# A decoder layer on one core: where the token numbers of the second choice are written

## The chip, the cores and the metric

The kernel runs on one core of a Trainium2 chip. The metric is the device time of one execution in microseconds (us); lower is better. The core's engines run side by side, each working through its own queue of instructions: TensorE (PE in the profile, with its weight loads as PEld), VectorE (DVE), ScalarE (ACT), GpSimd (POOL) and SyncE (SP), which issues DMAs. Engines wait for each other by semaphores.

## The reference

The input `x` is 64 sequences of 128 tokens with 256 features each. One layer does three things, with a layer normalization after each: a selective-scan block, a cross attention without softmax against `ctx_1024`, and a mixture of experts. Only the last matters here:

```python
shared = ...                                   # one expert that every token uses
probs = jax.nn.sigmoid(logits)                 # 8 experts
scores, indices = jax.lax.top_k(probs, TOP_K)  # the best 2
scores = scores / jnp.sum(scores, axis=-1, keepdims=True)
...
g = jax.nn.silu(jnp.einsum('th,ehi->tei', xf, gate_w))
u = jnp.einsum('th,ehi->tei', xf, up_w)
combined = jnp.einsum('tei,eih,te->th', g * u, down_w, w)
return shared + combined.reshape(b, s, h)
```

Every token thus has a first and a second choice of expert, and a weight for each.

## The kernel before

All values are 32-bit floats. The sequences are handled in 16 groups of 4 (`GB`), counted from 0; a group is 512 tokens, laid out as 128 partitions by 4 sequences.

For each group the program runs `front` and `scan` (the selective scan), then, while the next group's `front` and `scan` run, `after` (output projection, layernorm, cross attention, layernorm) and `route`. A weaver takes steps of these generators in turn, together with `early_shared` (the shared expert for an earlier group) and `routed` (tiles of rows for the eight routed experts). When the groups are through, the remaining routed tiles, the shared expert of groups 7 to 13 and the final sums follow.

`route` sorts tokens to experts. It computes the rank of each expert for each token ("gt", "same", "rank"), the position of each token in its expert's list ("pre", "count", "pc", "ad", "at", "index"), and the two weights ("wk2", "tot"). A token's features then go out twice, once for each choice, as rows of 258 numbers (`DX`): 256 features, in column `D` a number that says where its result is to be written later, in column `D + 1` the weight. `rows[0]` is the buffer in which `after` has already made x2; it comes from a ring of two and is called "x" or "x2" in the profile. `rows[1]` is "row1", a pool tile with one buffer, called "row" in the profile. (The profile also has a small tile "row" in the lists of tiles, L1139 to L1144, that has nothing to do with it.) Line 1016 copies x2 into row1 on ScalarE, line 1037 writes column `D` of both rows from a constant "slot", line 1038 writes column `D + 1`. Line 1042 scatters the rows to the DRAM tensor "xs": four indirect DMAs for each choice, issued by GpSimd, eight for each group.

The number in column `D` of a token at partition p of sequence b is 256 b + 2 p for the first choice and one more for the second.

The expert stage fetches tiles of 256 or 128 such rows (`fetch`, L1183), multiplies them with the gate and up weights (L663), forms "hid" (L1221, L1222), multiplies with the down weights (L672) and scatters the results to "ys" by the number in column `D` (L1235).

The order in which each engine gets its instructions isn't the program's. A planner simulates the engines, takes whatever it holds to be ready, and among ready ones the earlier in the program; buffers are handed out in the same way, and it puts in the semaphores. So an instruction with few dependencies can stand far ahead of its neighbours in the source. Within one engine the resulting order is then fixed: an instruction that waits holds up all behind it.

Other lines that the prediction names: L630 to L640 are the layernorm (statistics on VectorE, "rstd" on GpSimd, "shift" on VectorE, the scaling on ScalarE); L649 and L651 transpose; L672 is `project_rows`, used for the output projection from "sz" among others; L788 to L826 are the scan, with "d", "cj" and "mt" made on VectorE; L840 to L847 are its last products, with "sz" as their result; L868 adds the residual; L1065 and L1073 belong to the shared expert; L1080 stores x2 with the shared expert's part to "x_rows", from which it is read back at the end.

Of the kernel before, what the change touches and what calls it, by code (L numbers as in the profile page):

```python
# [11 lines left out]
F32 = mybir.dt.float32  # L12
AF = mybir.ActivationFunctionType
ALU = mybir.AluOpType
AX = mybir.AxisListType

P = 128
L = 128
D = 256
# [10 lines left out]
GB = 4  # L30
# [467 lines left out]
def shared_decay(K):  # L498

    with ExitStack() as ctx:
        _shared_decay(ctx, K)


def _shared_decay(ctx, K):
    tc, nc = K.tc, K.tc.nc
    NG = K.x.shape[0] // GB
# [8 lines left out]
    const = ctx.enter_context(tc.tile_pool(name="masks", bufs=1))  # L518
# [53 lines left out]
    with nc.allow_non_contiguous_dma(reason="a vector over partitions, once"):  # L572
        for j in range(NB):
# [15 lines left out]
    nc.vector.memset(order[:, 1, :], 1.0)  # L589
    count = const.tile([P, NE], F32, name="count")  # L590
    nc.vector.memset(count, 0.0)
    slot = const.tile([P, NG * GB, 2], F32, name="slot")
    nc.gpsimd.iota(slot, pattern=[[2 * L, NG * GB], [1, 2]], base=0, channel_multiplier=2,
                   allow_small_or_imprecise_dtypes=True)


# [71 lines left out]
    def project_rows(ps, src, w, cols):  # L668

        chunks = len(src)  # L670
        for k in range(chunks):
            nc.tensor.matmul(ps, lhsT=src[k], rhs=w[:, k, cols], start=(k == 0), stop=(k == chunks - 1))  # L672
# [268 lines left out]
    def wrote(g, ins):  # L941

        tc.declare_no_dep(ins, group="scatters", reason="other rows")
        for k in range(len(BATCHES)):
            if needs(k) <= g:
                tc.declare_no_dep(ins, group=f"fetches{k}", reason="other rows")
        for group in ("scatters", f"scatters{g}"):
            tc.add_to_no_dep_group(group, ins)
        writers.append((g, ins.name))
# [13 lines left out]
    def turned(x2):  # L963
        x2T = two.tile([P, KD, T], F32, name="x2T")
        transposed(x2T, x2)
        return x2T

    def route(g, st):

        x2 = st["x2"]  # L970
        x2T = turned(x2)
        yield

        pr = pm.tile([P, GB, NE], F32, name="pm")
        for b in range(GB):
            project_rows(
                pr[:, b, :], [x2T[:, k, b * L : (b + 1) * L] for k in range(KD)], rw, slice(0, NE)
            )
        pb = small.tile([P, GB, NE], F32, name="pb", bufs=1)
        nc.vector.tensor_tensor(pb, pr, rb.unsqueeze(1).to_broadcast([P, GB, NE]), ALU.add)  # L980
        nc.scalar.activation(pb, pb, AF.Exp, scale=-1.0)
        yield
        nc.vector.tensor_scalar(pb, pb, 1.0, None, ALU.add)
        nc.vector.reciprocal(pb, pb)
        pj = pb.unsqueeze(2).to_broadcast([P, GB, NE, NE])
        pe = pb.unsqueeze(3).to_broadcast([P, GB, NE, NE])
        gt = small.tile([P, GB, NE, NE], F32, name="gt", bufs=1)
        eq = small.tile([P, GB, NE, NE], F32, name="same", bufs=1)
        nc.vector.tensor_tensor(gt, pj, pe, ALU.is_gt)
        nc.vector.tensor_tensor(eq, pj, pe, ALU.is_equal)  # L990
        nc.vector.tensor_tensor(
            eq.rearrange("p b e j -> p b (e j)"), eq.rearrange("p b e j -> p b (e j)"),
            bef.rearrange("p e j -> p (e j)").unsqueeze(1).to_broadcast([P, GB, NE * NE]), ALU.mult,
        )
        nc.vector.tensor_tensor(gt, gt, eq, ALU.add)
        rank = small.tile([P, GB, NE], F32, name="rank", bufs=1)
        nc.vector.tensor_reduce(rank, gt, AX.X, ALU.add)
        sel = small.tile([P, GB, NE], F32, name="sel", bufs=1)
        nc.vector.tensor_scalar(sel, rank, 1.5, None, ALU.is_lt)


        pre = small.tile([P, GB, NE], F32, name="pre", bufs=1)
        nc.vector.tensor_copy(pre[:, 0, :], count)
        for b in range(1, GB):
            nc.vector.tensor_tensor(pre[:, b, :], pre[:, b - 1, :], sel[:, b - 1, :], ALU.add)
        nc.vector.tensor_tensor(count, pre[:, GB - 1, :], sel[:, GB - 1, :], ALU.add)
        yield
        yield
        pc = pm.tile([P, GB, NE], F32, name="pm")
        pcf = pc.rearrange("p b e -> p (b e)")  # L1010
        nc.tensor.matmul(pcf, lhsT=upto, rhs=sel.rearrange("p b e -> p (b e)"), start=True, stop=False)
        nc.tensor.matmul(pcf, lhsT=ones, rhs=pre.rearrange("p b e -> p (b e)"), start=False, stop=True)
        yield

        rows = [st["row"], one.tile([P, GB, DX], F32, name="row1")]
        nc.scalar.copy(rows[1][:, :, 0:D], x2)
        mk = small.tile([P, GB, 2, NE], F32, name="mk", bufs=1)
        nc.vector.tensor_tensor(
            mk, rank.unsqueeze(2).to_broadcast([P, GB, 2, NE]),
            order.unsqueeze(1).to_broadcast([P, GB, 2, NE]), ALU.is_equal,  # L1020
        )
        ad = small.tile([P, GB, NE], F32, name="ad", bufs=1)
        nc.vector.tensor_tensor(ad, pc, begin.unsqueeze(1).to_broadcast([P, GB, NE]), ALU.add)
        ma = small.tile([P, GB, 2, NE], F32, name="ma", bufs=1)
        nc.vector.tensor_tensor(ma, mk, ad.unsqueeze(2).to_broadcast([P, GB, 2, NE]), ALU.mult)
        at = small.tile([P, GB, 2], F32, name="at", bufs=1)
        nc.vector.tensor_reduce(at, ma, AX.X, ALU.add)
        index = small.tile([P, GB, 2], mybir.dt.int32, name="index", bufs=2)
        nc.vector.tensor_copy(index, at)
        nc.vector.tensor_tensor(ma, mk, pb.unsqueeze(2).to_broadcast([P, GB, 2, NE]), ALU.mult)  # L1030
        wk2 = small.tile([P, GB, 2], F32, name="wk2", bufs=1)
        nc.vector.tensor_reduce(wk2, ma, AX.X, ALU.add)
        tot = small.tile([P, GB], F32, name="tot", bufs=1)
        nc.vector.tensor_reduce(tot, wk2, AX.X, ALU.add)
        nc.vector.reciprocal(tot, tot)
        for k in range(2):
            nc.vector.tensor_copy(rows[k][:, :, D], slot[:, g * GB : (g + 1) * GB, k])
            nc.vector.tensor_tensor(rows[k][:, :, D + 1], wk2[:, :, k], tot, ALU.mult)  # L1038
        yield
        for k in range(2):  # L1040
            for b in range(GB):
                s = nc.gpsimd.indirect_dma_start(  # L1042
                    out=xs, in_=rows[k][:, b, :], in_offset=None,
                    out_offset=bass.IndirectOffsetOnAxis(ap=index[:, b, k : k + 1], axis=0),
                )
                wrote(g, s.ins)
        yield
        if g in LATE:
            nc.sync.dma_start(out=x2_rows[g].rearrange("p (b d) -> p b d", d=D), in_=x2)
        st["x2T"] = x2T  # L1050
# [242 lines left out]
    def second_half(g, st):  # L1293
        yield from after(g, st)
        yield
        yield from route(g, st)
        for k, (groups, *_) in enumerate(BATCHES):
            if groups == g + 1:
                tile_list(k)

    states = [{} for _ in range(NG)]
    rows = routed()
# [219 lines left out]
```

## Time and profile before

| what | us |
|---|---|
| median of 3 timed runs | 2166.24 |
| their range | 2158.91 to 2171.72 |
| the profiled execution | 2132.54 |
| its span, first to last instruction | 2130.8 |
| TensorE busy, groups 1 and 2 (125 to 287 us) | 145.84 of 162 |
| TensorE busy, groups 9 to 14 (852 to 1449 us) | 579.67 of 597 |
| TensorE busy, routed tiles after the groups (1640 to 1931 us) | 278.70 of 291 |

The profile's stretches show three regimes. In the first groups, which have no routed tiles to work on yet, TensorE idles some 10% of the time. From group 8 on, the routed tiles fill it. At the end, routed tiles and the shared expert run alone.

Lines of the profile read like this: line of the code, engine, operation, tiles (written <- read), shape; then the number of such instructions, their busy time and mean, and how long the engine stood idle ahead of them and what ended that idle time. A gap on TensorE costs time as such; on another engine it does only if TensorE has to wait in turn.

### The profile page before, as it was taken

Reading aid. Unit: us, or ns where it says so; the run is one execution under the profiler, and the core shown is the slowest. Engines: PE = TensorE matmul, PEld = TensorE weight load, DVE = VectorE, ACT = ScalarE, POOL = GpSimd, SP = SyncE. Lnnn points to the kernel's source line nnn. Section 1 sums busy time; section 2 is a strip of 40 time slices with the busy share of each in tenths; the row PEclk is TensorE's granted clock in tenths of the full one; section 3 lists DMA queues with packets and bytes.
Section 4 is the critical chain, followed back from the end, with each engine's and each line's share of the span. In section 5 each row is a group of like instructions: output and inputs, shape, how many; then the busy total and the mean of one; then the engine's idle time right before and its main releaser. Section 6 shows DMA issues by size and latency. Waiting matters only on the chain.

```text
span 2130.8 us, 25083 instructions
## 1 busy us (share of the span) xinstructions
PE 1963.9 (92%) x8748; PEld 1419.6 (67%) x8748; DVE 1001.5 (47%) x2426; ACT 775.9 (36%) x1254; POOL 462.9 (22%) x669
## 2 busy tenths in 40 slices
PE   4789899999898999999999999999989999888987
PEld 1546565666666676867676767777666888885544
DVE  3665665765555565545555654554431111113563
ACT  2444344342424343444444353535221222222332
POOL 3021221211202131313131222213131222221010
PEclk9899999999999999999999999999999999999999
DMA  4111111412212133424243333334243456844660
GB/s 123 33 49 32 49 58 40 157 40 75 90 60 90 60 125 114 140 75 164 80 149 115 114 120 109 97 102 150 80 156 129 160 193 206 312 144 158 211 213 32
DMA packets 97384, 245.13 MB, mean 115 GB/s; under 512 B 22400, under 2 KB 58880, under 8 KB 88288
## 3 DMA queue, kind: packets, MB, share of 16 engines
q1 hardware_dynamic: 74128, 188.17, 26.8%
q0 software_dynamic: 17616, 52.46, 7.3%
q10 hardware_dynamic: 5504, 2.81, 0.5%
q8 instruction: 71, 1.16, 0.2%
q14 instruction: 65, 0.53, 0.1%
HBM read 202.62 MB, written 54.93 MB: 121 GB/s over the span
## 4 chain that ended last, share of the span: by engine, by line
PE 70%; DVE 9%; DMA 7%; ACT 5%; POOL 4%; issue 4%; SPq 0%; DVEq 0%; POOLq 0%; ACTq 0%
PE gu L663 24%; PE pm L672 17%; PE pm L663 15%; PE pm L717 2%; POOL xs L1042 2%; PE gu L672 2%; PE pm L649 2%; PE pm L840 2%; DMA xs<-row,index 1%; PE pm L914 1%; PE pm L927 1%; PE pm L1203 1%; DMA x_back<-x_rows 1%; POOL rstd L635 1%; DMA routed_w<-in_ffn_dram 1%
## 5 line engine op out<-in xcount | busy, mean ns | idle before, releaser
L663 PE MATMUL gu<-rows_T,routed_w 128*128 128x256 f32 (+1 forms) x2496 | 507.3, 354 | 9.0 <-ACT rows_T L1205 5.5
L663 PEld LDWEIGHTS gu<-rows_T,routed_w 128*128 128x128 f32 x2496 | 416.5, 191 | 75.6 <-issue 20.1
L672 PE MATMUL pm<-routed_w,hid 128*128 128x256 f32 x1080 | 252.3, 381 | 13.7 <-DVE hid L1222 12.8
L663 PE MATMUL gu<-x2T,shared_w 128*128 128x512 f32 x512 | 238.9, 614 | 16.4 <-DVE hid L1222 7.7
L1222 DVE TENSOR_TENSOR hid<-hid,gu 128x512 f32<-128x512 f32 x135 | 91.9, 685 | 335.0 <-PE gu L663 323.5
L663 PE MATMUL pm<-xnT,w_in_s 128*128 128x512 f32 x512 | 244.7, 604 | 0.7 <-ACT xnT L653 0.7
L672 PEld LDWEIGHTS pm<-routed_w,hid 128*128 128x128 f32 x1080 | 200.7, 190 | 49.4 <-DVE hid L1222 17.5
L1235 POOL DMA_INDIRECT ys<-rows_out,to x135 | 133.7, 991 | 346.8 <-ACT rows_out L1234 310.3
L663 PEld LDWEIGHTS gu<-x2T,shared_w 128*128 128x128 f32 x512 | 97.4, 196 | 132.0 <-issue 108.0
L1221 ACT ACTIVATE hid<-gu 128x512 f32<-128x512 f32 x135 | 80.5, 596 | 260.2 <-PE gu L663 259.9
L701 DVE SCALAR_TENSOR_TENSOR xc<-pm,cw,xc 128x508 f32<-128x508 f32 (+2 forms) x192 | 140.6, 740 | 65.6 <-ACT xc L696 62.5
L663 PEld LDWEIGHTS pm<-xnT,w_in_s 128*128 128x128 f32 x512 | 97.6, 195 | 86.1 <-issue 74.8
L1234 ACT ACTIVATE rows_out<-pm,wt 128x256 f32<-128x256 f32 x135 | 57.8, 471 | 266.3 <-PE pm L672 245.6
L635 POOL TENSOR_TENSOR rstd<-var,mhalf 128x4 f32<-128x4 f32 x64 | 68.1, 1065 | 346.6 <-DVE var L633 179.1
L672 PE MATMUL pm<-w_out_s,sz 128*128 128x256 f32 x512 | 121.7, 394 | 13.2 <-DVE sz L847 13.1
L672 PE MATMUL gu<-shared_w,hc 128*128 128x256 f32 x512 | 118.9, 382 | 5.5 <-DVE hc L1065 5.5
L672 PEld LDWEIGHTS pm<-w_out_s,sz 128*128 128x128 f32 x512 | 99.9, 198 | 31.9 <-DVE sz L847 16.3
L672 PEld LDWEIGHTS gu<-shared_w,hc 128*128 128x128 f32 x512 | 95.1, 190 | 27.4 <-DVE hc L1065 8.7
L1042 POOL DMA_INDIRECT xs<-x,index x64 | 66.2, 1034 | 126.3 <-DVE row L1038 49.5
L696 ACT ACTIVATE xc<-pm,cb,cw 128x512 f32<-128x512 f32 x64 | 49.5, 773 | 110.0 <-PE pm L663 110.0
L640 ACT ACTIVATE x<-x,shift,rstd 128x256 f32<-128x256 f32 x128 | 67.9, 590 | 57.3 <-DVE shift L637 57.3
L1205 ACT COPY rows_T<-pm 128x512 f32<-128x512 f32 (+1 forms) x78 | 41.2, 528 | 130.3 <-PE pm L1203 130.3
(225 smaller groups left out, 2628.4 us busy)
## 6 DMA issues: line engine op xcount, KB each, us to landing
routed_w<-in_ffn_dram SPq DMA_DIRECT2D x78, 1536.0 KB
picked<-ys SPq DMA_DIRECT2D x16, 1024.0 KB
rows_in<-xs SPq DMA_DIRECT2D x57, 258.0 KB
xt<-in_x_dram POOLq DMA_DIRECT2D x16, 512.0 KB, 4.3
cT<-in_ctxT_dram POOLq DMA_DIRECT2D x16, 512.0 KB, 4.2
cq<-chunks SPq DMA_DIRECT2D x16, 512.0 KB
x_rows<-x SPq DMA_DIRECT2D x16, 512.0 KB
x_back<-x_rows SPq DMA_DIRECT2D x16, 512.0 KB
```

The costliest lines, as they stand in the source:

```text
L635: nc.gpsimd.tensor_tensor(rstd, var, mhalf, ALU.pow)
L640: nc.scalar.activation(dst[:, b, :], src[:, b, :], AF.Identity, bias=shift[:, b : b + 1], scale=rstd[:, b : b + 1])
L649: nc.tensor.transpose(ps[:, b * L : (b + 1) * L], src[:, b, k * P : (k + 1) * P], ident)
L663: nc.tensor.matmul(ps, lhsT=w[:, k, col : col + P], rhs=src[:, k, :], start=(k == 0), stop=(k == KD - 1),)
L672: nc.tensor.matmul(ps, lhsT=src[k], rhs=w[:, k, cols], start=(k == 0), stop=(k == chunks - 1))
L696: nc.scalar.activation(xcf[:, c, :], ps, AF.Identity, bias=cb[:, c : c + 1], scale=cw[:, c, TAPS - 1 : TAPS],)
L701: nc.vector.scalar_tensor_tensor(xc[:, c, :, s:], ps3[:, :, : L - s], cw[:, c, TAPS - 1 - s : TAPS - s], xc[:, c, :, s:], ALU.mult, ALU.add,)
L1042: s = nc.gpsimd.indirect_dma_start(out=xs, in_=rows[k][:, b, :], in_offset=None, out_offset=bass.IndirectOffsetOnAxis(ap=index[:, b, k : k ...
L1221: nc.scalar.activation(hc, psg, AF.Silu)
L1222: nc.vector.tensor_tensor(hc, hc, psu, ALU.mult)
L1234: nc.scalar.activation(y[:, j, :], ps[:, j, :], AF.Copy, scale=wt[:, j : j + 1])
L1235: s = nc.gpsimd.indirect_dma_start(out=ys, in_=y[:, j, :], in_offset=None, out_offset=bass.IndirectOffsetOnAxis(ap=to[:, j : j + 1], axis=0),)
```

## The change

The constant "slot" holds the numbers of the first choice alone. They are copied into column `D` of `rows[0]` ahead of the copy of x2. ScalarE's copy into row1 takes 257 columns in place of 256, so that it carries the first choice's number along, and VectorE adds 1 to it in row1. What is computed stays the same.

```diff
-    slot = const.tile([P, NG * GB, 2], F32, name="slot")
-    nc.gpsimd.iota(slot, pattern=[[2 * L, NG * GB], [1, 2]], base=0, channel_multiplier=2,
+    slot = const.tile([P, NG * GB], F32, name="slot")
+    nc.gpsimd.iota(slot, pattern=[[2 * L, NG * GB]], base=0, channel_multiplier=2,
                    allow_small_or_imprecise_dtypes=True)
...
         rows = [st["row"], one.tile([P, GB, DX], F32, name="row1")]
-        nc.scalar.copy(rows[1][:, :, 0:D], x2)
+        nc.vector.tensor_copy(rows[0][:, :, D], slot[:, g * GB : (g + 1) * GB])
+        nc.scalar.copy(rows[1][:, :, 0 : D + 1], rows[0][:, :, 0 : D + 1])
...
         nc.vector.reciprocal(tot, tot)
+        nc.vector.tensor_scalar(rows[1][:, :, D], rows[1][:, :, D], 1.0, None, ALU.add)
         for k in range(2):
-            nc.vector.tensor_copy(rows[k][:, :, D], slot[:, g * GB : (g + 1) * GB, k])
             nc.vector.tensor_tensor(rows[k][:, :, D + 1], wk2[:, :, k], tot, ALU.mult)
```

## The prediction

> **What bounds the kernel now.** I read the page first, then the table of waits over all engines, then the waits of TensorE alone, then the lines that the diff touches, and last the timeline around each of them.
>
> The page's first part says who is busy:
>
> ```profile
> PE 1963.9 (92%) x8748; PEld 1419.6 (67%) x8748; DVE 1001.5 (47%) x2426; ACT 775.9 (36%) x1254; POOL 462.9 (22%) x669
> ```
>
> TensorE has work for 92% of the span of 2130.8 us, so about 167 us is all that any other engine can still be costing. A gain has to come out of those 167 us. The table of waits shows one wait that belongs to a line of the diff (columns: who waited, for whom, total us, times, longest us):
>
> ```profile
> DVE hid L1222 <- PE gu L663: 323.5, 88, 7.2
> ...
> DVE row L1037 <- DMA xs<-row,index: 137.9, 15, 14.0
> ```
>
> The first row is VectorE waiting for the bottleneck, which is healthy. The second is not: a copy of four numbers for each partition holds VectorE still for 137.9 us, 15 times, until the scatter DMAs that read "row" have landed. L1037 copies the token numbers from the constant "slot" into column D of both rows. The constant is ready from the start, so nothing but the buffer holds this copy back, and it stands far ahead of the routing it belongs to: in group 2 it runs at 240.9 us, while "mk" (L1018) of that group runs at 296.1. "row1" has one buffer, which the eight scatters of the group before are still reading. TensorE's own waits on VectorE:
>
> ```profile
> PE pm L788 <- DVE d L784: 19.0, 12, 4.9
> PE pm L672 <- DVE sz L847: 13.1, 5, 6.1
> ...
> PE pm L840 <- DVE mt L826: 12.4, 4, 5.7
> ```
>
> To see which of these are caused by L1037 I went through the timeline at each of the 15 places. Groups are counted from 0. Group 1, group 6 and group 9 (start, us, engine, line, idle before and its releaser):
>
> ```profile
> 156.38 0.96 POOL L1042 DMA_INDIRECT xs<-row,index  x1 [0.30 <-issue]
> 158.97 0.17 DVE L1037 COPY row<-slot 128x4 f32<-128x4 f32 x1 [5.60 <-DMA xs<-row,index]
> 159.05 0.69 DVE L847 TENSOR_TENSOR sz<-sz,xc 128x512 f32<-128x512 f32 x1
> 159.79 1.65 PE L672 MATMUL pm<-w_out_s,sz 128*128 128x256 f32 x3 [5.41 <-DVE sz L847]
> ```
>
> ```profile
> 571.51 1.89 PE L663 MATMUL gu<-rows_T,routed_w 128*128 128x256 f32 x8
> 579.00 1.41 PE L840 MATMUL pm<-mt,xd 128*128 128x128 f32 x5 [5.60 <-DVE mt L826]
> ...
> 578.06 0.17 DVE L1037 COPY row<-slot 128x4 f32<-128x4 f32 x1 [10.05 <-DMA xs<-row,index]
> 578.16 0.69 DVE L826 TENSOR_TENSOR mt<-mt,pm 128x512 f32<-128x512 f32 x1
> ```
>
> ```profile
> 890.69 5.35 PE L663 MATMUL gu<-rows_T,routed_w 128*128 128x256 f32 x24
> ...
> 894.42 0.17 DVE L1037 COPY row<-slot 128x4 f32<-128x4 f32 x1 [12.44 <-DMA xs<-row,index]
> ```
>
> In groups 1 and 6 the instruction right behind the copy in VectorE's queue is the one TensorE needs next. In group 9 the stall is longer still, but TensorE is filled with matmuls of the routed experts throughout.
>
> **What the Trainium skill says.** "TensorE: Matmul & The Clock Gate", table at the top: VectorE's and ScalarE's queues are strict FIFO. The trace agrees: L847 does not run while L1037 waits. "DMA: Bandwidth & Descriptors", section on the SWDGE path: a fixed cost of about 2.0 us, most of it the receipt for the last byte. Here the last scatter of group 1 is issued at 156.38 and releases the copy at 158.97, 2.6 us later. "Perfetto Trace Analysis", section Optimization Strategy: find the gaps of the bound engine and what blocks them; the sum below is made that way.
>
> **The change, part by part.**
>
> *Removed: the copy into "row" column D.* Its wait for the scatters goes with it. The other copy, into "x" (the group's own row, two buffers), stays, and is as early as before: its waits are 2.2 us in all (1.7 and 0.5). What the removal is worth to TensorE I take from TensorE's gaps at the stalls (us): group 1, 5.41; group 2, 6.14; group 3, 2.12 and 0.83 (transposes at L649 waiting for the layernorm that began behind the copy); group 5, 0.68 and 0.70; group 6, 5.60; group 7, 5.74; group 15, 0.83. Sum 28.05. In group 4 TensorE waits 3.70 us right after the stall, but for the fetch of routed rows, which SyncE issues after the scatters; I count nothing. In groups 8 to 14 the seven stalls sum to 74.6 us and TensorE waits for none of them: nothing there either. So of 137.9 us, 28 us are on the path.
>
> What is late next? Group 1: L847 would start at 153.37 and end at 154.06; TensorE is done with its earlier work at 159.79 - 5.41 = 154.38, so the gap closes entirely. Group 6: "mt" would be ready at 568.7, and TensorE comes free at 573.4: closed. Group 3: the second half of the projection ends at 320.3; in the trace the transpose starts 3.88 us after that half's L868, so at 324.2, and TensorE is busy to 325.2: closed. I keep 1 us back for the places where VectorE and TensorE end within 0.4 us of each other (five, at 0.2 us each).
>
> *Moved: the copy of x2 to row1 on ScalarE (L1016)* reads one column more and now also depends on the copy from "slot". It grows from 128x1024 to 128x1028 elements: 4/1024 of its 1047 ns, 16 times, 0.07 us. Its new wait costs nothing: the copy from "slot" runs 47 to 149 us earlier (group 2: 219.7 against 286.8). It was already waiting for the scatters of the group before (two semaphore instructions of 38 ns ahead of it), and these have landed at least 41 us before. It cannot run ahead as L1037 did, since it reads x2, which the layernorm finishes just then.
>
> *Added: the +1 on VectorE.* One TENSOR_SCALAR of 128x4, 0.17 us like L763, in place of one COPY of 0.17 us (median 172 ns): nothing. Its wait is new: it needs the ScalarE copy. If it stands as early as possible, it holds VectorE until that copy ends. In groups 0 to 2 VectorE has at most two small operations there (L729, L752), and in groups 3 to 14 it has nothing to do then: group 8's copy ends at 853.45 and VectorE's next instruction, "hid", starts at 854.59 after an idle 2.77 us, waiting for TensorE. Over the groups this reserve is 1.1 to 4.4 us. Cost between 0 and, if ScalarE's copy comes some 2 us later than this reserve in every group, 2 x 16 = 32 us; I take 0. Behind it would be queued "hc", "hid" and "tok", which TensorE's down projections and ScalarE wait for. If it stands where the program puts it, after the reciprocal, the copy is done 10 us earlier and there is no wait at all.
>
> *Moved: nothing on SyncE or POOL.* The scatters still wait for L1038. The constant is half as wide, at start-up only.
>
> Sum: -28.05 + 0.07 + 1 = -27 us, from 2132.5 (the profiled execution) to 2105.5. The timed runs shown have a median of 2166.24 (2158.91 to 2171.72), 1.6% above the profiled one; the gaps are waiting times, so I carry the difference in us: 2166.2 - 27 = 2139.
>
> **What I can't see.** The order on each engine is laid out by a planner, and another instruction list gives another order. Downwards: the small gaps before L788 (19.0 us, 4.9 of them in the first group) may close too: 28 + 14 = 42 us, 2124; runs of one kernel spread by 6 us around their median, so I go to 2120. Upwards, the rivals set the end.
>
> **Rivals.**
>
> *A, the stall goes and stays gone:* 2139. For it: the seven places above, with the next instruction named at each.
>
> *B, another copy takes its place:* the copy "x" from "slot" is also unbound and stands near the old one (group 5: 480.8, held 0.89 us by the x_rows store; the other at 486.9). With VectorE earlier, it may come before that store has landed; group 2's store takes 5.7 us to land (213.95 to 219.63). At 3 us in each of groups 2 to 8, 21 of the 28 us come back: 2166 - 7 = 2159. Against it: in groups 1 to 5 and 8 it stands ahead of the old copy, so no stall of that group shields it, and in 6 and 7 the store itself is issued behind the old stall (579.48), so it moves forward with it. That the change does not lift the wait at all belongs here: the buffer's scatters would then hold ScalarE, but long after they landed.
>
> *C, slower: VectorE is held by the +1.* Place: the end of the layernorm of x2 in each group, if the planner puts the +1 early and ScalarE takes the copy behind other work. Price: a hold that reaches TensorE like those of groups 6 and 7, 5.6 us; in seven groups 39 us, so 2166 - 28 + 39 = 2177. It decides from 28/16 = 1.75 us lost on TensorE in every group. Against it: the reserve above, and that stalls of 12 us in groups 8 to 14 cost nothing.
>
> **How the numbers follow.** A change below 0.5% (11 us) is what a measurement of this kernel can't tell from none. A 0.75, B 0.13, C 0.12. Of A, 0.73 lie beyond 0.5% and 0.02 within; of B, 0.04 beyond and 0.09 within; of C, 0.11 slower and 0.01 within. Faster 0.77, same 0.12, slower 0.11. The range is 2120 to 2161: A with its unknown order, and most of B; C and the tails are left out.
>
> **What would show it.** After: no row "DVE row <- DMA xs<-row,index" in the waits; TensorE's waits for "sz" at about 0.2 us (13.1 less 12.93) and for "mt" at about 1.1 (12.4 less 11.34); TensorE's busy time unchanged at about 1964 us and its share up to 93%; groups 8 to 14 still about 99 us long, groups 1 to 7 shorter by 28 us together. Wrong would be: a wait of VectorE for the ScalarE copy row<-x, longer waits for x_rows, or gaps on TensorE at places that have none now.

## The result

Timed beside each other, the changed kernel takes 2130.05 us (median of 4 runs, 2126.02 to 2133.43) and the kernel before 2162.57 us (4 runs, 2155.16 to 2171.72). The ratio is 0.9847, 95% interval 0.9802 to 0.9892: 32.5 us less, where 27 were forecast. The profiled execution took 2126.02 us, its span is 2124.3.

After the change, the first part of the page:

```profile
PE 1962.0 (92%) x8748; PEld 1421.2 (67%) x8748; DVE 1005.6 (47%) x2426; ACT 775.6 (37%) x1254; POOL 462.2 (22%) x669
```

After the change, from the table of waits over all engines (who waited, for whom, total us, times, longest us):

```profile
DVE hid L1223 <- PE gu L663: 317.8, 94, 7.2
...
DVE row L1037 <- ACT row L1017: 23.6, 15, 3.7
```

And from the waits of TensorE alone:

```profile
PE gu L663 <- ACT rows_T L1206: 25.6, 15, 7.2
PE pm L788 <- DVE d L784: 21.3, 13, 4.9
...
PE pm L840 <- DVE mt L826: 1.1, 2, 0.6
```

VectorE's 137.9 us of waiting for the scatters are gone. In their place stands a wait of 23.6 us, that of the +1 (now L1037) for ScalarE's copy (now L1017). On TensorE the wait for "sz" is gone and that for "mt" is down from 12.4 to 1.1 us. But there is a new row at the top: TensorE waits 25.6 us for "rows_T", against 5.5 before. It looks as if the change had paid with a new wait. Several of the experiments below ask whether it has.

The order of instructions is the same in both kernels on TensorE, ScalarE, GpSimd and SyncE, from first to last. On VectorE the only differences are that the sixteen early copies "row" from "slot" are gone and sixteen +1 have come, each right behind ScalarE's copy. So the planner did not answer with another order; what changed is when things run.

Here the span is cut at the starts of ScalarE's copy to row1 of groups 0, 7 and 14, into groups 1 to 7, groups 8 to 14, and the rest. The columns are the stretch in us, its length, then busy us (and number of instructions) of PE, PEld, DVE, ACT and POOL, the granted clock (the share of its full clock that TensorE was given), the DMA share and GB/s. Before:

```profile
125.00:749.00 624.00, 584.87 (x2409) 386.67 (x2410) 369.76 (x886) 244.57 (x381) 123.28 (x141) 0.98 0.22 68
749.00:1449.00 700.00, 681.49 (x3137) 510.51 (x3136) 373.44 (x907) 310.95 (x480) 178.62 (x243) 1.00 0.36 116
1449.00:2130.00 681.00, 618.13 (x2939) 477.93 (x2937) 198.66 (x488) 177.73 (x333) 134.64 (x237) 0.97 0.48 165
```

After:

```profile
122.00:710.00 588.00, 573.40 (x2412) 379.75 (x2413) 370.98 (x886) 244.53 (x380) 122.80 (x140) 0.99 0.23 72
710.00:1438.00 728.00, 691.42 (x3139) 517.44 (x3137) 376.12 (x907) 312.11 (x483) 179.12 (x243) 0.98 0.34 112
1438.00:2124.00 686.00, 618.78 (x2937) 480.44 (x2936) 199.53 (x489) 176.90 (x332) 134.62 (x237) 0.97 0.48 164
```

Groups 1 to 7 are 36 us shorter, more than the 28 us forecast for them, and groups 8 to 14 are 28 us longer, where no difference was forecast. Two questions follow: why is the gain in the early groups larger than the gaps that were counted, and what do the late groups pay for?

### The profile page after: what moved, and what is told of

Same layout as the page of the kernel before. It is cut to its first block, busy times and chain, and to the rows that moved or that the text cites. A ratio compares the mean times of both kernels' runs of the same rounds, so it can differ in the third digit from the quotient of the medians.

```text
span 2124.3 us, 25079 instructions
## 1 busy us (share of the span) xinstructions
PE 1962.0 (92%) x8748; PEld 1421.2 (67%) x8748; DVE 1005.6 (47%) x2426; ACT 775.6 (37%) x1254; POOL 462.2 (22%) x669
## 4 chain that ended last, share of the span: by engine, by line
PE 71%; DVE 9%; issue 5%; ACT 5%; DMA 5%; POOL 2%; another core or an unknown queue 1%; SPq 0%; POOLq 0%; DVEq 0%; ACTq 0%
PE gu L663 24%; PE pm L672 16%; PE pm L663 15%; PE gu L672 3%; PE pm L840 2%; PE pm L717 2%; PE pm L649 2%; PE pm L914 1%; PE pm L927 1%; PE pm L1204 1%; POOL rstd L635 1%; PE pm L833 1%; PE pm L802 1%; DMA ys<-rows_out,to 1%
## 5 line engine op out<-in xcount | busy, mean ns | idle before, releaser
L663 PE MATMUL gu<-rows_T,routed_w 128*128 128x256 f32 (+1 forms) x2496 | 514.4, 358 | 28.4 <-ACT rows_T L1206 25.6
L672 PE MATMUL gu<-shared_w,hc 128*128 128x256 f32 x512 | 123.3, 392 | 15.0 <-DVE hc L1066 9.7
L672 PE MATMUL pm<-w_out_s,sz 128*128 128x256 f32 x512 | 114.8, 380 | 0.3 <-issue 0.2
L844 DVE SCALAR_TENSOR_TENSOR xc<-xc,dsk,pm 128x512 f32<-128x512 f32 x64 | 46.9, 742 | 88.6 <-PE pm L840 55.5
```

The lines of the kernel that those rows point to most:

```text
L663: nc.tensor.matmul(ps, lhsT=w[:, k, col : col + P], rhs=src[:, k, :], start=(k == 0), stop=(k == KD - 1),)
L844: nc.vector.scalar_tensor_tensor(y, xcf[:, c, :], dsk[:, c : c + 1], ps.rearrange("p b l -> p (b l)"), ALU.mult, ALU.add)
```

## The experiments

They ran on three chips, on each beside runs of the kernel before, whose median was 2162.5 us on the first, 2158.62 on the second and 2135.5 on the third. Ratios are to the kernel before on the same chip.

**First chip: both kernels again, the stall put back, and the bound copy.** The kernel before, unchanged:

> The kernel before, unchanged, for a profile from the same chip as the three runs after it, and for the noise. All theories: ratio 1.000 within 0.5%. The theory of the prediction (seven of the fifteen stalls reach TensorE, 28 us, and the seven of groups 8 to 14 cost nothing): groups 1 to 7 take some 624 us and groups 8 to 14 some 701 us, as in the profile before. Rival (groups 8 to 14 are not free, the profile before was a lucky execution in which they were covered): groups 8 to 14 take over 715 us here, with gaps of TensorE behind the copies row<-slot.

The changed kernel, unchanged:

> The changed kernel, unchanged. Measured once at 0.9847, so 0.98 to 0.99. Theory of the prediction: groups 1 to 7 some 588 us, about 36 us shorter than before: 28 us of gaps and some 8 us because TensorE's granted clock falls to half for 5 to 6 us behind each gap, which the prediction left out; groups 8 to 14 within 5 us of before on this chip. Rival (a real cost of the change in groups 8 to 14, as the first pair of profiles suggests): groups 8 to 14 some 27 us longer than before on this chip too.

Measured: 2162.73 us, ratio 1.0007 (0.9988 to 1.0026), and 2127.04 us, 0.9831 (0.98 to 0.9862). Kernel before, groups 1 to 7 and 8 to 14, columns as above:

```profile
123.00:750.00 627.00, 587.17 (x2413) 388.86 (x2414) 371.02 (x886) 245.09 (x382) 123.45 (x141) 0.97 0.22 68
750.00:1476.00 726.00, 693.08 (x3138) 519.27 (x3136) 377.14 (x907) 311.22 (x482) 176.47 (x243) 0.98 0.35 112
```

The changed kernel on the same chip:

```profile
121.50:708.00 586.50, 573.00 (x2413) 379.52 (x2414) 371.13 (x886) 244.81 (x382) 123.29 (x140) 1.00 0.23 72
708.00:1441.00 733.00, 692.53 (x3137) 518.58 (x3136) 377.33 (x907) 311.29 (x481) 178.10 (x243) 0.98 0.34 111
```

The kernel before, too, needs 726 us for groups 8 to 14 here, where its first profile shows 700. Most of what looked like the price of the change comes without the change. The first two profiles were apparently of chips that differ, and comparing them puts 26 to 28 us of this difference on the change. Not quite all is explained: the changed kernel's 733 us are 7 us more than 726, past the 5 us allowed for in the expectation, and the rest of its span is 3 us longer. So some 10 of the 40.5 us that groups 1 to 7 gain are lost again later on this chip. One profile of each kernel can't tell whether the change does that; the third chip, below, bears on it.

Next, the changed kernel with a copy that waits for the scatters as the old one did. It writes column D + 1, which is written again later:

```diff
         nc.vector.tensor_copy(rows[0][:, :, D], slot[:, g * GB : (g + 1) * GB])
+        nc.vector.tensor_copy(rows[1][:, :, D + 1], slot[:, g * GB : (g + 1) * GB])
         nc.scalar.copy(rows[1][:, :, 0 : D + 1], rows[0][:, :, 0 : D + 1])
```

> The changed kernel with the wait put back alone: VectorE copies slot into column D + 1 of row1 (overwritten later by the weight), a copy that nothing but the buffer holds back. Theory of the prediction: the whole gain goes, ratio 1.000 within 0.5%, and VectorE waits some 138 us for the scatters again. Rival (the gain is from the changed copy of ScalarE or from fewer early instructions): ratio stays at 0.985.

Measured: 2162.62 us, 0.9998 (0.9985 to 1.0012). From the table of waits over all engines:

```profile
DVE row L1017 <- DMA xs<-row,index: 138.3, 15, 14.2
```

One copy with that wait takes the whole gain away, with the +1, the wider copy and the small constant all still in place. So it is the stall that the gain comes from, and the other parts of the change neither add to it nor take from it by more than the interval allows.

The other way round: the kernel before with only its copy for row1 bound to late data, so that it can't stand early. "tot" is ready only after the reciprocal, and 0 x tot + slot is the number wanted:

```diff
-            nc.vector.tensor_copy(rows[k][:, :, D], slot[:, g * GB : (g + 1) * GB, k])
+            if k:
+                nc.vector.scalar_tensor_tensor(rows[1][:, :, D], tot, 0.0, slot[:, g * GB : (g + 1) * GB, 1], ALU.mult, ALU.add)
+            else:
+                nc.vector.tensor_copy(rows[0][:, :, D], slot[:, g * GB : (g + 1) * GB, 0])
```

> The kernel before with only the early copy into row1 undone: column D of row1 is written as tot * 0 + slot, so it can't stand ahead of the weights; ScalarE's copy stays at 256 columns and there is no +1 and no wait of VectorE for ScalarE. Theory of the prediction (all of the gain is the wait for the scatters, the rest of the change is free): the same time as the changed kernel, ratio 0.985. Rival (a part of the change's own work costs time in groups 8 to 14): faster than the changed kernel by up to 27 us, ratio 0.972 to 0.978.

Measured: 2140.08 us, 0.9885 (0.9859 to 0.991): less of a gain than the change brings, by 13 us, which neither of the two theories had expected. In its profile the difference stands in groups 8 to 14, which take 742 us against 733; groups 1 to 7 take 589 against 586.5. This raised the question whether the wider ScalarE copy or the +1 has a merit of its own.

**Second chip: where the stall costs, and where the 13 us come from.** The copy that brings the stall back, in the early groups alone, and in another kernel, with `g >= 8` in place of `g < 8`, in the late ones alone:

```diff
+        if g < 8:
+            nc.vector.tensor_copy(rows[1][:, :, D + 1], slot[:, g * GB : (g + 1) * GB])
```

> The changed kernel with the wait put back in groups 1 to 7 alone (the copy of slot into column D + 1 of row1 for groups below 8). Theory of the prediction (only these stalls reach TensorE): the whole gain goes, 2162 us within 8. Rival (the stalls of all groups cost, about half in each half): some 2145 us.

> The changed kernel with the wait put back in groups 8 to 15 alone. Theory of the prediction (stalls of some 12 us in these groups are covered by the matmuls of the routed tiles): as the changed kernel, 2127 us within 8, though VectorE waits some 75 to 90 us for the scatters again. Rival: some 2145 us.

Stall in groups 1 to 7: 2160.11 us, 1.001 (0.9998 to 1.0022). Its row in the waits, and its groups 1 to 7 in the stretches:

```profile
DVE row L1018 <- DMA xs<-row,index: 49.6, 7, 10.2
```

```profile
123.00:749.00 626.00, 585.80 (x2411) 388.10 (x2410) 370.95 (x893) 244.63 (x380) 123.57 (x140) 0.97 0.21 68
```

Stall in groups 8 to 15: 2117.4 us, 0.981 (0.9797 to 0.9823). The same two views:

```profile
DVE row L1018 <- DMA xs<-row,index: 88.1, 8, 13.6
```

```profile
120.00:707.00 587.00, 572.98 (x2414) 379.86 (x2415) 372.28 (x886) 245.49 (x382) 124.26 (x141) 1.00 0.23 72
```

The larger part of the waiting, 88.1 us, costs nothing: this kernel gains as much as the two below, which have no such wait at all. The smaller part, 49.6 us, costs all of it, 42.7 us between the two kernels. The table of waits ranks them the other way. And look at the busy time of TensorE in groups 1 to 7: 585.80 us with the stall, 572.98 without, for the same matmuls at a granted clock of 0.97 and 1.00.

Then the bound copy in two forms, each shown against the bound copy above: with ScalarE's copy over 257 columns as in the change, and bound to a column of x2 in place of "tot":

```diff
-        nc.scalar.copy(rows[1][:, :, 0:D], x2)
+        nc.vector.tensor_copy(rows[0][:, :, D], slot[:, g * GB : (g + 1) * GB, 0])
+        nc.scalar.copy(rows[1][:, :, 0 : D + 1], rows[0][:, :, 0 : D + 1])
...
-            else:
-                nc.vector.tensor_copy(rows[0][:, :, D], slot[:, g * GB : (g + 1) * GB, 0])
```

> e3_bound_late with ScalarE's copy over 257 columns that reads the copy from slot, as in the changed kernel; VectorE still overwrites column D late. It took 13 us more than the changed kernel. If that is because the write of column D stands late, between the weights that the scatters wait for: 2140 us again. If it is because of ScalarE's shorter copy or its place: 2127 us.

```diff
-                nc.vector.scalar_tensor_tensor(rows[1][:, :, D], tot, 0.0, slot[:, g * GB : (g + 1) * GB, 1], ALU.mult, ALU.add)
+                nc.vector.scalar_tensor_tensor(rows[1][:, :, D], rows[0][:, :, 0], 0.0, slot[:, g * GB : (g + 1) * GB, 1], ALU.mult, ALU.add)
```

> e3_bound_late with column D of row1 written as x2 * 0 + slot: bound to the end of the layernorm in place of the weights, so that it stands where the changed kernel has its +1, but reads nothing of ScalarE's copy into row1. If the wait of VectorE for ScalarE's copy (23.6 us in the changed kernel's first profile) costs nothing, as predicted: 2127 us within 6, as the changed kernel. If it costs: faster than the changed kernel by 5 us or more. If every kernel without the +1 has e3's 13 us: 2140 us.

Measured: 2120.87 us, 0.982 (0.9806 to 0.9835), and 2118.83 us, 0.9825 (0.9811 to 0.9839). The kernel that stalls late alone, with the +1, and these two without it gain the same. The times in us that the expectations name come from the first chip, and the changed kernel itself was not timed on the second, so it ran again on the third.

**Third chip: the 13 us again, and the wait on another engine.** The kernel bound to "tot" once more, and the changed kernel once more:

> e3_bound_late once more, unchanged: 0.9885 in its first run, while e9 and e10, which differ from it by one instruction each, gave 0.982. If the 13 us belong to this kernel's instructions: 0.9885 within 0.3% again. If they belong to the chip or the hour: 0.982 to 0.984.

> The changed kernel beside it on the same chip: 0.981 to 0.986. If e6, e9 and e10 are no better than the change, it is as they were, 0.981 to 0.983; if they are, it stays at 0.9835 to 0.986.

Measured: 2096.84 us, 0.9817 (0.9796 to 0.9838), and 2094.03 us, 0.9813 (0.979 to 0.9836). Side by side they differ by 2.8 us, inside their intervals. The 13 us did not come back. Why they showed on the first chip is open. The wider copy and the +1 show no merit of their own on the second and the third chip.

The changed kernel on this chip, the three stretches:

```profile
122.00:708.00 586.00, 571.65 (x2414) 379.03 (x2415) 371.25 (x887) 245.86 (x383) 123.36 (x141) 1.00 0.23 73
708.00:1408.00 700.00, 680.22 (x3138) 509.65 (x3135) 376.13 (x907) 311.39 (x481) 181.68 (x243) 1.00 0.36 116
1408.00:2090.00 682.00, 618.50 (x2937) 480.38 (x2936) 199.10 (x489) 176.86 (x332) 135.59 (x237) 0.97 0.49 165
```

Beside the first profile of before this is the picture the prediction drew, apart from the size of the early gain: groups 8 to 14 at 700 us in both, the rest at 681 and 682, groups 1 to 7 at 624 and 586. The kernel before was timed on the third chip, but not profiled there, so these two profiles are of the same chip or of one like it only by inference: the first profile's execution took 2132.54 us, as runs of the kernel before do on the third chip (2131.14 to 2143.02). And TensorE's waits here:

```profile
PE pm L788 <- DVE d L784: 21.0, 13, 4.9
...
PE gu L663 <- ACT rows_T L1206: 5.4, 8, 0.7
```

The 25.6 us for "rows_T" are 5.4 here, with the same kernel.

Last, the same number made on ScalarE: row1's column D as x's column plus a constant 1, right behind the copy in the source, with no +1 on VectorE. If the planner places it early, its wait for the scatters of the group before lies on ScalarE, with other work queued behind it:

```diff
-        nc.scalar.copy(rows[1][:, :, 0 : D + 1], rows[0][:, :, 0 : D + 1])
+        nc.scalar.copy(rows[1][:, :, 0:D], x2)
+        nc.scalar.activation(rows[1][:, :, D], rows[0][:, :, D], AF.Identity, bias=ones[:, 0:1])
...
-        nc.vector.tensor_scalar(rows[1][:, :, D], rows[1][:, :, D], 1.0, None, ALU.add)
```

> The +1 moved to ScalarE as an instruction of its own that reads the first row's number and writes column D of row1, so that nothing but the buffer holds it back: the planner puts it far ahead of the copy, and the wait for the scatters of the group before moves from VectorE to ScalarE. Theory of the prediction (what costs is an engine held in its queue with work behind it that TensorE needs): waits of ScalarE for the scatters appear, and at least 15 us of the gain go, 2140 us or more, depending on what stands behind the instruction on ScalarE. If only VectorE's stall matters: 2120 to 2127 us.

Measured: 2171.36 us, 1.0173 (1.0151 to 1.0195): 77 us above the changed kernel and slower than before. From its waits over all engines, ScalarE's timeline in group 9 and TensorE's beside it (start, us, engine, line, idle before and its releaser):

```profile
ACT row L1018 <- DMA xs<-row,index: 132.2, 14, 12.2
```

```profile
854.59 0.30 ACT L1018 ACTIVATE row<-x,ones 128x4 f32<-128x4 f32 x1 [11.54 <-DMA xs<-row,index]
855.50 0.58 ACT L1206 COPY rows_T<-pm 128x512 f32<-128x512 f32 x1
```

```profile
856.14 3.78 PE L663 MATMUL gu<-rows_T,routed_w 128*128 128x256 f32 x8 [8.61 <-ACT rows_T L1206]
```

Nearly the same 132 to 138 us of waiting, now in ScalarE's queue. Behind it stands the copy of "rows_T" that the routed tiles' matmuls need, and TensorE stands still for 8.61 us. Over the whole span TensorE waits 63.2 us for "rows_T", against 5.4 in the changed kernel. Groups 1 to 7, which lost from the stall on VectorE, lose nothing here (586 us). Groups 9 to 15, which had lost nothing, lose 7 to 13 us each, and group 8 about 2.

A second buffer for row1, which would take the wait itself away, was not tried.

## Why the prediction was right, point by point

**The cause.** Right: the copy that nothing but its buffer held back. Putting the wait back gives 0.9998, and binding the copy to late data gives the gain without any other part of the change. That only the early groups pay was right as well: all of the price comes with 49.6 us of the stall and none with the other 88.1.

**"So of 137.9 us, 28 us are on the path."** This is the term that was mis-sized. The gain was 32.5 us in the first measurement, 35.5 on the first chip and 41.5 on the third. The two kernels on the second chip that stall early and late show what it consists of: in groups 1 to 7 TensorE idles 40.2 us with the stall (626 - 585.80) and 14.0 without (587 - 572.98), so 26.2 us, close to the 27 us of gaps that the prediction added up for these groups. And it is busy 12.8 us less for the same matmuls. The first profile of before against the changed kernel on the third chip says the same: 24.8 us of idle time and 13.2 us of busy time in these groups. The prediction took TensorE's busy time to be fixed, and that step failed.

That 32.5 us came so near the forecast is partly luck: on the first chip groups 1 to 7 gain 40.5 us, and some 10 us are lost later in the span, which the prediction had not foreseen either.

Why the busy time isn't fixed shows just behind the place where the prediction's own quotation ended. Kernel before, TensorE's timeline in group 1, the whole run of matmuls behind the gap:

```profile
159.79 7.35 PE L672 MATMUL pm<-w_out_s,sz 128*128 128x256 f32 x20 [5.41 <-DVE sz L847]
```

The same twenty in the changed kernel on the third chip, where there is no gap:

```profile
152.37 4.52 PE L672 MATMUL pm<-w_out_s,sz 128*128 128x256 f32 x20
```

And the granted clock of the kernel before in three stretches: the gap, and the time behind it (the third number from the right):

```profile
154.40:159.80 5.40, 0.01 (x1) 0.01 (x1) 0.76 (x2) 0.00 (x0) 2.33 (x3) 0.89 0.22 77
159.80:162.00 2.20, 2.20 (x5) 1.84 (x6) 0.00 (x0) 0.00 (x0) 0.00 (x0) 0.50 0.00 0
162.00:165.00 3.00, 3.00 (x8) 2.36 (x7) 0.54 (x1) 0.00 (x0) 0.00 (x0) 0.50 0.00 0
```

Behind the gap TensorE runs at half its clock for over 5 us, so a gap of 5.41 us costs 5.41 + (7.35 - 4.52) = 8.2 us. The Trainium skill says so in kind, in "TensorE: Matmul & The Clock Gate", Part 1, The HAM clock gate: after an idle window of about 3.4 us the clock falls to half, and it takes about as long of sustained work to come back. The prediction named this page, but for the queues alone. The trace agrees on the fall, with 0.50 behind a gap of 5.41 us. The return took longer than the page says: work began at 159.79, and at 165.00 the clock was still at 0.50.

The trace of the kernel before has six such spells at a clock of 0.50 in groups 1 to 7; the changed kernel on the third chip has none there. They last 6.8 us at the gaps of groups 1, 2 and 7 and 3.4 us in groups 3, 4 and 6. If half of TensorE's busy time in a spell counts as lost, they cost an estimated 2.8, 2.8, 1.9, 1.7, 1.7 and 1.4 us in this order, 12.3 us of the 13.2. So the price of a gap is not fixed. In group 3 the idle time ahead was 2.12 and 0.83 us, with 0.8 us between them, so gaps shorter than the page's 3.4 us can be enough when they lie close together. In group 4 it was the wait of 3.70 us for the fetch, which the prediction counted at nothing; the changed kernel on the third chip has a gap of 3.67 us there too, and keeps its clock.

**What is late next.** As forecast, nothing of size: TensorE's wait for "sz" is gone (about 0.2 us expected) and that for "mt" is 1.1 us (1.1 expected).

**The +1.** The price of zero was right, though not by the safer of the two ways. The planner put it as early as possible, and the wait that the prediction named as a sign of error, VectorE for ScalarE's copy, is there: 23.6 us, 15 times. It fits into the reserve, 1.1 to 4.4 us in each group, that the prediction had read from the idle time before "hid"; the longest wait is 3.7 us. The kernel bound to "tot" has no such wait and the one bound to x2 one of 10.0 us, and they are not faster: 2096.84 us against 2094.03 for the changed kernel on the third chip, and 2118.83 against 2117.4 for the kernel with the +1 and the late stall on the second.

**The wider copy.** From the changed kernel's instructions on the third chip, by line (least, median, greatest ns, first and last start in us):

```profile
L1017 ACT COPY row<-x x16: 1036/1048/1053, 122.5 to 1503.9; 128x1028 f32<-128x1028 f32 x16
```

1048 ns against 1047: nothing, as forecast.

**The rivals.** B, the copy to "x" held by the store to x_rows: its waits are 1.9 us there, against 2.2 before. C, slower by a hold that reaches TensorE: not on VectorE with the +1. But a hold that does reach TensorE was seen on another engine: on ScalarE, whose copies feed the routed tiles, it costs 77 us.

**"What I can't see."** The new order that the downward end of the range allowed for did not come. The waits before L788 stayed (19.0 before, 21.0 and 21.3 after). The gain beyond 27 us comes with TensorE's busy time, as shown above, and not from these gaps.

**The check that misled.** "Groups 8 to 14 still about 99 us long" and "TensorE's busy time unchanged at about 1964 us" were to tell right from wrong. The first profile of after gave 104 us for each group, as if the first were wrong, and 1962.0, as if the second were right. On the third chip it is 100 us and 1948.8. Between the first two profiles two effects cancelled, one of the stall and one mostly of the chips: TensorE was busy 11.5 us less in the early groups (584.87 to 573.40) and 9.9 us more in the late ones (681.49 to 691.42).

## What to carry to other kernels

An instruction whose only dependency is its buffer was placed early by this planner, and it then holds an in-order engine for as long as the buffer's readers take; give it an input that comes late, here the row itself, and it can no longer stand where it hurts. What a wait costs is not read from its length but from what is queued behind it: of nearly 138 us of waiting on VectorE, the 88.1 us in the late groups were worth nothing and the 49.6 us in the early ones some 40, while 132.2 us on ScalarE cost 77. A gap on TensorE can cost more than its length: here 26.2 us of gaps came with 12.8 us of slower work. And a stretch that gets longer in a profile is to be looked for in the old kernel, on the same chip, before the change is charged with it.

## What the runs showed of the hardware

The kernel before takes 2135.5 us on one chip and 2158.62 and 2162.5 on two others. For the changed kernel, profiled on the first chip and on the third, 33 of the 37 us between the two spans lie in groups 8 to 14, where a group's scatters run beside routed tiles. The changed kernel on the first chip, TensorE and then VectorE some 35 us after group 11's copy to row1 (timeline):

```profile
1164.02 1.06 PE L840 MATMUL pm<-mt,xd 128*128 128x128 f32 x8
...
1172.32 3.78 PE L663 MATMUL gu<-rows_T,routed_w 128*128 128x256 f32 x8 [7.24 <-ACT rows_T L1206]
```

```profile
1171.60 0.75 DVE L844 SCALAR_TENSOR_TENSOR xc<-xc,dsk,pm 128x512 f32<-128x512 f32 x1 [9.03 <-remote]
```

The same place on the third chip:

```profile
1142.97 1.06 PE L840 MATMUL pm<-mt,xd 128*128 128x128 f32 x8
...
1143.87 1.94 PE L663 MATMUL gu<-rows_T,routed_w 128*128 128x256 f32 x8
```

On the first chip the products of L840 are recorded as ended at 1165.08 (the profile models the ends of matmuls), yet VectorE, which waits for them, goes on only at 1171.60: 6.5 us during which the record shows no work in the way. TensorE then waits 7.24 us, and its next eight matmuls take 3.78 us in place of 1.94. This is what stands behind "PE gu <- ACT rows_T" in the first profile of after, and the kernel before has it on that chip as well (21.8 us).

The profile calls the releaser of such waits "remote", that is, another core or an unknown queue. On VectorE and ScalarE they add up to 35.3 us in the kernel before on the first chip, to 64.5 in the changed kernel and to 79.0 in the one bound to "tot", and in this order groups 8 to 14 take 726, 733 and 742 us there. On the second chip they are 30 to 35 us; in the three profiles from the third chip there are none. That the 13 us and the 7 us on the first chip come from these delays would fit, but with one profile of each it is not shown, and what causes the delays was not settled.
